# Image-prompt keys projected standing beside the values, then transposed, in a cross-attention kernel

## Chip, cores and metric

The kernel runs on one NeuronCore of one Trainium2 chip. The metric is the device time of one execution in microseconds (us), as the median of several runs; lower is better. Everything is float32. The engines are named as in the profile: PE is the matrix engine (TensorE), PEld its weight loads, DVE the vector engine, ACT the scalar engine, POOL is GpSimd, SP the queue that issues most DMAs.

## What is computed

The reference is one cross-attention layer with image prompts, over a batch of B = 8, with S = 112 queries of C = 320 channels, 20 heads of 16 channels, and a context of T = 375 rows of E = 512 of which the last 4 are image prompts:

```python
text_ehs = encoder_hidden_states[:, :-NUM_TOKENS]
ip_ehs = encoder_hidden_states[:, -NUM_TOKENS:]
q = heads(hidden_states @ W_q)
k_t = heads(text_ehs @ W_k)
v_t = heads(text_ehs @ W_v)
scores_t = jnp.einsum('bhsd,bhtd->bhst', q, k_t) * attn_scale
probs_t = jax.nn.softmax(scores_t, axis=-1)
text_out = jnp.einsum('bhst,bhtd->bhsd', probs_t, v_t)
...
k_ip = heads(ip_ehs @ W_k_ip)
v_ip = heads(ip_ehs @ W_v_ip)
attn_scores = jnp.einsum('bhsd,bhnd->bhsn', q, k_ip) * attn_scale
qsem = jnp.einsum('bhst,bte->bhse', probs_t, text_ehs)
qsem = _l2norm(qsem)
ip_n = _l2norm(ip_ehs)
sem = jnp.einsum('bhse,bne->bhsn', qsem, ip_n)
fused = attn_scores + SEM_SCALE * sem
probs_ip = jax.nn.softmax(fused, axis=-1)
probs_ip = probs_ip * spatial_mask[None, None, :, None]
ip_out = jnp.einsum('bhsn,bhnd->bhsd', probs_ip, v_ip)
...
out = text_out + IP_SCALE * ip_out
out = out @ W_out + b_out
out = out + residual
```

The change concerns only `k_ip` and `v_ip`: the 8 x 4 = 32 prompt rows of all batch items (512 long) times two weights of 512 x 320. Both are computed once, for the whole batch.

## The kernel before

The heads are handled in groups of four (`GROUP`), five groups (`NG`) for each batch item `b`, so there are 40 steps `(b, g)`. A prologue loads and prepares batch item 0. Then the main loop runs over the steps. In a step, `multiplied` issues twelve rounds (`j`) of four matmuls, one for each head of the group, each on its own 32 rows of the array (L673). Between its rounds the scores of the group two steps ahead are computed (`scores`, L624), and the four of them are turned into probabilities (`probabilities`: DVE maximum L637, ACT exponential L641, and a DMA from SP, L646, that lays them out for the DVE transposition of L654, which makes the stationary operand of the following step). The text values and the Gram matrix of the context come in as the moving operand `u`, which SP fills from the doubled Gram matrix (`gram_to_groups`, L460) and POOL with the values (`placed`, L591).

After the rounds, `between(b, g)` issues what prepares the next batch item: the Gram matrix ("inner products") of its context in three blocks of shrinking width (`gram`, L446, 375, 247 and 119 columns, each copied out by ACT at L434), its values (L518), keys (L484), queries (L326). At `b == 0` and `g == 0` it also issues `prompt_projections`, right behind the third block of `gram(1)`.

The order of the instructions of PE, SP, DVE and, in the main loop, ACT is the order of the program text (`manual_schedule`); POOL's is left to a scheduler until the last batch item. The tiles of one tag rotate through their buffers: `bank()` takes one of two banks of PSUM (tag "mm"), so that a tile can only be written when the tile before the last has been read out.

`prompt_projections` before the change works on `ipT`, the 32 prompts standing as columns (four chunks of 128 rows x 32). For the keys, `wkip_sb` is the stationary operand, 128 x 128 at a time: three blocks `i` of output channels by four chunks `e`, each with the 32 prompts as the moving operand (L270). Each block's result, channels x prompts, is copied by ACT into `kip` (L277), and DVE spreads batch item 0's part by heads into `kipb` (L278). The channels of the last block are set apart first, with 16 zeros after each 16 channels, by `spread` on POOL (three copies, L122, and a memset, L123), for which `wkip_sb` is 384 wide. For the values, `ipT` is the stationary operand, 128 x 32, and the 320 channels are the moving one (L287), so that the result stands as prompts x channels; ACT copies it into `vip` (L291), and in step (0, 1) SP sends it to DRAM (`vipd`, L294), from where each batch item's rows are later read back. `kip` is used by `keys(b)` (a POOL copy, L468), and `kipb` by `prompt_logits(0)` in step (0, 3).

Both weights lie in one buffer of the tag "u" (`wip`), which batch item 1's `u` takes over later; they are loaded by two DMAs on SP (L1078 and L1079, recorded under the helper's L116) at the end of the prologue.

Of the kernel before, what the change touches and what calls it, by code (L numbers as in the profile page):

```python
# [8 lines left out]
F32 = mybir.dt.float32  # L9
# [11 lines left out]
def kernel(  # L21
# [14 lines left out]
    nc = tc.nc  # L36
    P = 128
    B, S, C = x.shape
    T, E = ehs.shape[1:]
    H = HEADS  # L40
    D = C // H
# [3 lines left out]
    NE = E // P  # L45
    HC = P // D
    NC = (C + P - 1) // P
    CP = NC * P
    FULL = C // P
# [7 lines left out]
    N = B * NIP  # L57
# [18 lines left out]
    work = ctx.enter_context(tc.tile_pool(name="work", bufs=2))  # L76
# [6 lines left out]
    def bank(name, spare=False):  # L83

        if spare:
            return ps_sc.tile([P, 512], F32, tag="sc", name=name)
        return ps_mm.tile([P, 512], F32, tag="mm", name=name)
# [13 lines left out]
    wv_sb = const.tile([P, NE, C + REST], F32, tag="wv_sb", name="wv_sb")  # L101

    wip = work.tile([P, UCOL], F32, tag="u", name="wip")
    wkip_sb = wip[:, : NE * CP].rearrange("p (e f) -> p e f", f=CP)
    wvip_sb = wip[:, NE * CP : NE * (CP + C)].rearrange("p (e f) -> p e f", f=C)
    wo_sb = const.tile([P, NC, C], F32, tag="wo_sb", name="wo_sb")
    ip_sb = const.tile([N, E], F32, tag="ip_sb", name="ip_sb")
    sm_sb = const.tile([S, 1], F32, tag="sm_sb", name="sm_sb")
# [9 lines left out]
    def spread(eng, t):  # L118

        v = t[:, :, FULL * P :].rearrange("p k (a r d) -> p k a r d", r=2, d=D)  # L120
        for a in (3, 2, 1):
            eng.tensor_copy(v[:, :, a, 0, :], v[:, :, a // 2, a % 2, :])  # L122
        eng.memset(v[:, :, :, 1, :], 0.0)  # L123
# [43 lines left out]
    ident = const.tile([P, P], F32, tag="ident", name="ident")  # L167
# [46 lines left out]
    ipT = const.tile([P, NE, N], F32, tag="ipT", name="ipT")  # L214
    ipnT = const.tile([P, NE, N], F32, tag="ipnT", name="ipnT")
    kip = const.tile([P, NC, N], F32, tag="kip", name="kip")

    kipb = const.tile([P, NC, HC, NIP], F32, tag="kipb", name="kipb")
    vipd = dram.tile([N, C], F32, tag="vipd", name="vipd", bufs=1)
# [43 lines left out]

    def prompt_projections():

        spread(nc.gpsimd, wkip_sb)
        for i in range(NC):
            ps = bank(f"ps_kip{i}")
            for e in range(NE):
                nc.tensor.matmul(  # L270
                    ps[:, :N],
                    wkip_sb[:, e, i * P : (i + 1) * P],
                    ipT[:, e, :],
                    start=(e == 0),
                    stop=(e == NE - 1),
                )
            nc.scalar.copy(kip[:, i, :], ps[:, :N])  # L277
            nc.vector.tensor_tensor(  # L278
                kipb[:, i],
                kip[:, i, :NIP].unsqueeze(1).to_broadcast([P, HC, NIP]),  # L280
                hmask.unsqueeze(2).to_broadcast([P, HC, NIP]),
                ALU.mult,
            )
            yield
        ps = bank("ps_vip")
        for e in range(NE):
            nc.tensor.matmul(  # L287
                ps[:N, :C], ipT[:, e, :], wvip_sb[:, e, :], start=(e == 0), stop=(e == NE - 1)
            )
        vip = work.tile([N, C], F32, tag="vip", name="vip", bufs=1)  # L290
        nc.scalar.copy(vip, ps[:N, :C])  # L291
        yield

        nc.sync.dma_start(vipd, vip)  # L294
        yield


# [131 lines left out]
    def doubled(ps, c):  # L429

        t0 = c * P
        k = min(P, TT - t0)
        g = ug[:, GCOL[c] : GCOL[c] + T - t0]
        nc.scalar.mul(g, ps[:, : T - t0], 2.0)  # L434
        nc.gpsimd.tensor_tensor(g[:, :k], g[:, :k], half[:, :k], ALU.mult)

    def gram(b):

        ctxT = st[b]["ctxT"]

        nc.gpsimd.tensor_copy(ctxT[:, :, TT:T], ipnT[:, :, b * NIP : (b + 1) * NIP])
        for c in range(NT):
            t0 = c * P
            ps = bank(f"ps_g_{b}_{c}")
            for e in range(NE):
                nc.tensor.matmul(  # L446
                    ps[:, : T - t0],
                    ctxT[:, e, t0 : t0 + P],
                    ctxT[:, e, t0:T],
                    start=(e == 0),  # L450
                    stop=(e == NE - 1),
                )
            doubled(ps, c)
            yield
# [536 lines left out]
    def run(key, make, pieces=1):  # L991

        if key not in gens:
            gens[key] = make()
        for _ in range(pieces):
            next(gens[key], None)

    def between(b, g):

        nb = b + 1  # L1000
        new = nb < B


        first = [bs for bs in pairs if bs[0] == (nb if b == 0 else nb + 1)]
        rest = [bs for bs in pairs if bs[0] == nb]
        if g == 0:
            if new:
                run(("g", nb), lambda: gram(nb), 3)
            if b == 0:
                run(("pp",), prompt_projections, NC + 1)  # L1010
            if b > 0 and new:
                run(("f", b - 1), lambda: finish(b - 1))
        if g == 1:
            if new:
                run(("v", nb), lambda: values(nb), 2)
            for bs in first if b == 0 else ():
                run(("q", bs[0]), lambda: project_queries(bs), 3)
        if g == 2 and new:
            run(("v", nb), None)
            run(("k", nb), lambda: keys(nb))  # L1020
            for bs in first if b == 0 else ():
                run(("q", bs[0]), None)
        if g == 2 and b > 0 and new:
            run(("f", b - 1), None, 2)
        if g == 3:
            if new:
                run(("k", nb), None, 1)
            if b > 0 and new:
                run(("f", b - 1), None)
            for bs in first if b > 0 else ():  # L1030
                run(("q", bs[0]), lambda: project_queries(bs), 3)
            if b == 0:
                run(("t", b), lambda: prompt_logits(b))
            for bs in rest:
                run(("q", bs[0]), None)
        if 0 <= g - (b == 0) < NT and nb + 1 < B:
            run(("c", nb + 1), lambda: transposed_context(nb + 1))
        if g == 4:
            if b > 0 and new:
                run(("f", b - 1), None, 2)  # L1040
            if nb < B - 1:
                run(("k", nb), None, 1)
            for bs in (first if b > 0 else []) + rest:
                run(("q", bs[0]), None)
# [49 lines left out]
    for n, (b, g) in enumerate(steps[:-NG]):  # L1094
# [41 lines left out]
        if g == NG - 1 and b < B - 2:  # L1136
            prompt_values(b)
        between(b, g)
        if g == 1:
            values_to_dram(b + 1, nc.sync, 0, 2)  # L1140
# [12 lines left out]
    b = B - 1  # L1153
# [12 lines left out]
    for g in range(NG):  # L1166
# [20 lines left out]
        if g < NG - 1:  # L1187

            n = GROUP - 1 if g <= LEAD else 1
# [36 lines left out]
    last = last_heads(b)  # L1226
# [52 lines left out]
```

## Time and profile before

| what | value |
|---|---|
| median of 3 runs | 442.44 us |
| lowest and highest run | 440.67, 444.03 us |
| profiled execution, first to last instruction | 442.3 us, at a mean granted PE clock of 0.998 |
| DVE, ACT, POOL busy | 325.5, 189.0, 111.7 us |
| rounds of `multiplied`, L673 | 3840 records, 220.5 us of the span |
| DMA | 64.22 MB, mean 145 GB/s |

Of the profiled execution the span is what is recorded; it stands 0.1 us below the median of the runs. In the trace one float32 matmul appears as two records, one for each pass, and a transposition by PE as one. The records of PE overlap, because a matmul's end is modelled and the next one starts before it: what a matmul costs is the distance from one start to the next, not its duration. A shape such as "128*32 128x320" reads: 128 rows and 32 columns of the array, and a moving operand of 128 x 320.

### The profile page before, as it was taken

How to read it: one execution, taken by the hardware profiler on the slowest of the kernel's cores; microseconds unless marked ns; L12 is line 12 of the kernel's file. 1: busy time of each engine (PE TensorE's matmuls, PEld its weight loads, DVE VectorE, ACT ScalarE, POOL GpSimd, SP SyncE). 2: the span in 40 equal slices, each digit the busy share in tenths (PEclk: the TensorE clock that was granted, in tenths of full speed). 3: DMA queues.
4: the chain of work that ended last, by engine and by line, in shares of the span. 5: the costliest groups of instructions: out<-in, count | busy, mean ns of one | idle time of the engine just before them, and what ended most of it. 6: DMA issues, size and time to landing. Idle time of an engine off the chain costs nothing.

```text
span 442.3 us, 12958 instructions
## 1 busy us (share of the span) xinstructions
PE 429.4 (97%) x5024; PEld 330.7 (75%) x5024; DVE 325.5 (74%) x664; ACT 189.0 (43%) x649; POOL 111.7 (25%) x270
## 2 busy tenths in 40 slices
PE   8998999989999999999999999999999999999896
PEld 8857767778777877788777787778777887776784
DVE  4046366886897877887797977977787687878874
ACT  2263233343534353333633453333534253436783
POOL 5302201011142121511142120602124111526440
PEclk9999999999999999999999999999999999999999
DMA  8569965466646756468646746468465527553300
GB/s 249 151 173 254 220 147 151 110 152 126 165 122 166 178 121 162 129 155 159 165 115 163 183 110 164 113 144 199 116 175 139 152 77 197 130 146 105 83 13 27
DMA packets 57995, 64.22 MB, mean 145 GB/s; under 512 B 18432, under 2 KB 52088, under 8 KB 57934
## 3 DMA queue, kind: packets, MB, share of 16 engines
q1 hardware_dynamic: 57494, 62.83, 57.0%
q8 instruction: 40, 0.66, 0.7%
q10 hardware_dynamic: 440, 0.56, 0.4%
q14 instruction: 21, 0.17, 0.1%
HBM read 18.67 MB, written 5.32 MB: 54 GB/s over the span
## 4 chain that ended last, share of the span: by engine, by line
PE 88%; ACT 3%; DMA 3%; DVE 3%; issue 1%; POOL 1%; SPq 0%; POOLq 0%; DVEq 0%
PE ps_qd L673 39%; PE ps_v L518 14%; PE ps_k L484 10%; PE ps_g L446 8%; PE ps_s L624 4%; PE ps_q L326 3%; DMA xg<-p 2%; PE ps_o L883 2%; PE ps_g L418 1%; DVE xgT L654 1%; PE ps_c L388 1%; ACT p L641 1%; PE ps_k L500 1%; DMA ct<-in_ctx_dram 1%; POOL shared L708 1%
## 5 line engine op out<-in xcount | busy, mean ns | idle before, releaser
L673 PE MATMUL ps_qd<-u,xgT 32*112 32x72 f32 (+11 forms) x3840 | 220.5, 353 | 3.2 <-DVE xgT L654 1.3
L673 PEld LDWEIGHTS ps_qd<-u,xgT 32*112 32x112 f32 x3840 | 187.5, 172 | 37.0 <-issue 10.7
L654 DVE STREAM_TRANSPOSE xgT<-xg 128x1536 f32<-128x1536 f32 x40 | 119.1, 2979 | 12.1 <-DMA xg<-p 8.2
L641 ACT ACTIVATE p<-ps_s,nmx 112x371 f32<-112x371 f32 x160 | 87.3, 584 | 86.2 <-DVE nmx L637 69.6
L637 DVE TENSOR_REDUCE nmx<-ps_s 112x1 f32<-112x371 f32 x160 | 77.6, 527 | 50.8 <-PE ps_s L624 49.7
L719 DVE CUSTOM_DVE_ANT_0 junk<-ps_qd,p 112x371 f32<-112x371 f32 x148 | 80.2, 542 | 15.6 <-ACT vext L525 0.5
L624 PE MATMUL ps_s<-kT,qm 32*112 32x375 f32 (+1 forms) x320 | 67.8, 484 | 0.4 <-ACT p L641 0.4
L591 POOL COPY u<-vr 128x64 f32<-128x64 f32 x120 | 25.9, 238 | 151.9 <-PE ps_qd L673 102.3
L518 PE MATMUL ps_v<-wv_sb,ctxT 128*128 128x384 f32 (+1 forms) x192 | 63.5, 480 | 0.0
L518 PEld LDWEIGHTS ps_v<-wv_sb,ctxT 128*128 128x128 f32 x192 | 35.2, 190 | 19.7
L484 PE MATMUL ps_k<-ctxT,wk_sb 128*128 128x371 f32 x136 | 45.9, 482 | 0.0
L686 ACT COPY pvs<-ps_qd 112x21 f32<-112x21 f32 x150 | 16.0, 189 | 65.7 <-PE ps_qd L673 64.8
L446 PE MATMUL ps_g<-ctxT 128*128 128x375 f32 (+2 forms) x168 | 37.6, 380 | 0.0
L484 PEld LDWEIGHTS ps_k<-ctxT,wk_sb 128*128 128x128 f32 x136 | 25.1, 190 | 15.3 <-issue 0.5
L446 PEld LDWEIGHTS ps_g<-ctxT 128*128 128x128 f32 x168 | 28.0, 190 | 8.7 <-ACT ug L434 0.3
L624 PEld LDWEIGHTS ps_s<-kT,qm 32*112 32x112 f32 x320 | 27.1, 170 | 6.3 <-ACT kT L491 2.1
L335 DVE TENSOR_SCALAR qm<-ps_q,emask 128x224 f32<-128x224 f32 (+1 forms) x25 | 9.1, 397 | 20.2 <-PE ps_q L326 20.1
L643 ACT COPY ipl<-ps_s 112x4 f32<-112x4 f32 x140 | 23.8, 170 | 0.0
L525 ACT COPY vext<-ps_v 128x384 f32<-128x384 f32 (+1 forms) x24 | 11.2, 468 | 25.6 <-PE ps_v L518 25.6
L378 DVE STREAM_TRANSPOSE ctxT<-ct 128x512 f32<-128x512 f32 x18 | 19.8, 1103 | 0.1
L491 ACT COPY kT<-ps_k 128x371 f32<-128x371 f32 x17 | 8.0, 469 | 25.3 <-PE ps_k L484 25.3
L858 POOL TENSOR_TENSOR wv<-vip,w 112x1280 f32<-112x1280 f32 x6 | 14.8, 2466 | 15.0 <-DVE w L802 15.0
(160 smaller groups left out, 319.8 us busy)
## 6 DMA issues: line engine op xcount, KB each, us to landing
xg<-p SPq DMA_DIRECT2D x160, 162.3 KB
u<-ug SPq DMA_DIRECT2D x128, 99.0 KB
ct<-in_ctx_dram SPq DMA_DIRECT2D x24, 176.0 KB
vr<-vd SPq DMA_DIRECT2D x32, 120.0 KB
vip<-vipd SPq DMA_DIRECT2D x6, 560.0 KB
vd<-vext SPq DMA_DIRECT2D x7, 320.0 KB
vd<-vext SPq DMA_DIRECT2D x7, 160.0 KB
out_dram<-ob SPq DMA_DIRECT2D x8, 140.0 KB
```

The source lines that it names most:

```text
L378: nc.vector.transpose(ctxT[:, :, c * P : (c + 1) * P].rearrange("p e (j i) -> p j e i", i=RG), ct[:, some, :].rearrange("p j (k e) -> p j ...
L446: nc.tensor.matmul(ps[:, : T - t0], ctxT[:, e, t0 : t0 + P], ctxT[:, e, t0:T], start=(e == 0), stop=(e == NE - 1),)
L484: nc.tensor.matmul(ps[:, :TT], wk_sb[:, e, i * P : (i + 1) * P], s["ctxT"][:, e, :TT], start=(e == 0), stop=(e == NE - 1),)
L518: nc.tensor.matmul(ps[:, :w], ctxT[:, e, c * P : (c + 1) * P], wv_sb[:, e, :w], start=(e == 0), stop=(e == NE - 1),)
L591: nc.gpsimd.tensor_copy(region(b, c)[:, :, UV - c * P :], s["vr"][:, c * QN : (c + 1) * QN, g, :])
L624: nc.tensor.matmul(ps[:S, :w], qm[a * RG : (a + 1) * RG, i, r, j * S : (j + 1) * S], s["kT"][a * RG : (a + 1) * RG, i, :w], start=True, st ...
L637: nc.vector.tensor_reduce(nmx, ps[:S, :TT], AX.X, ALU.max, negate=True)
L641: nc.scalar.activation(p, ps[:S, :TT], AF.Exp, bias=nmx)
L643: nc.scalar.copy(s["ipl"][:, groups[g][a], :], ps[:S, TT:T])
L654: nc.vector.transpose(xT.rearrange("p j (k q) -> p q j k", q=QN), xg.rearrange("p q (j k) -> p q j k", k=RG),)
L673: nc.tensor.matmul(banks[a][:S, j * RG : UW], xT[a * RG : (a + 1) * RG, j, :S], region(b, c)[a * RG : (a + 1) * RG, q, q * RG :], start=(j ...
L719: nc.vector.tensor_tensor_reduce(out=junk, in0=ps[:S, :TT], in1=s["p", g][:, a, :], scale=1.0, scalar=0.0, op0=ALU.mult, op1=ALU.add, accu ...
```

## The change

The keys are projected the way the values are, with the prompts as the stationary operand, and both at once: chunk by chunk, one matmul for the keys into the PSUM partitions 0 to 31 of a bank and one for the values into the partitions 32 to 63 of the same bank, which are two different groups of 32 columns of the array. ACT copies the keys out in two pieces, the second of which sets the last block's channels apart (the zeros between them are written by POOL into the tile `both` beforehand), and the values in a third. Then three PE transpositions, of 32 x 128 each, bring the keys to channels x prompts in one bank, one ACT copy takes them to `kip`, and three DVE instructions make `kipb` as before. `spread` of the weight falls away, and the key weight is 320 wide, loaded as one piece for each partition instead of four.

In `between(0, 0)` the order becomes: two blocks of `gram(1)`, the projections and their three copies, the third block of `gram(1)`, then the transpositions, the copy and the three DVE instructions. The transfer to `vipd` stays in step (0, 1). POOL's scheduler puts the new memset near the start of the program, between the first two instructions that make the identity matrix.

```diff
-    wkip_sb = wip[:, : NE * CP].rearrange("p (e f) -> p e f", f=CP)
-    wvip_sb = wip[:, NE * CP : NE * (CP + C)].rearrange("p (e f) -> p e f", f=C)
+    wkip_sb = wip[:, : NE * C].rearrange("p (e f) -> p e f", f=C)
+    wvip_sb = wip[:, NE * C : 2 * NE * C].rearrange("p (e f) -> p e f", f=C)
...
-        spread(nc.gpsimd, wkip_sb)
-        for i in range(NC):
-            ps = bank(f"ps_kip{i}")
-            for e in range(NE):
+        both = work.tile([2 * N, CP], F32, tag="ipkv", name="ipkv", bufs=1)
+        kp = both[:N]
+        last = kp[:, FULL * P :].rearrange("n (a r d) -> n a r d", r=2, d=D)
+        nc.gpsimd.memset(last[:, :, 1, :], 0.0)
+        ps = bank("ps_ipkv")
+        for e in range(NE):
+            for i, w in enumerate((wkip_sb, wvip_sb)):
                 nc.tensor.matmul(
-                    ps[:, :N],
-                    wkip_sb[:, e, i * P : (i + 1) * P],
+                    ps[i * N : (i + 1) * N, :C],
                     ipT[:, e, :],
+                    w[:, e, :],
                     start=(e == 0),
                     stop=(e == NE - 1),
                 )
-            nc.scalar.copy(kip[:, i, :], ps[:, :N])
+        nc.scalar.copy(kp[:, : FULL * P], ps[:N, : FULL * P])
+        nc.scalar.copy(
+            last[:, :, 0, :], ps[:N, FULL * P : C].rearrange("n (a d) -> n a d", d=D)
+        )
+        nc.scalar.copy(both[N : 2 * N, :C], ps[N : 2 * N, :C])
+        yield
+
+        ps = bank("ps_kip")
+        for i in range(NC):
+            nc.tensor.transpose(
+                ps[:, i * N : (i + 1) * N], kp[:, i * P : (i + 1) * P], ident[:N, :N]
+            )
+        nc.scalar.copy(kip, ps[:, : NC * N].rearrange("p (i n) -> p i n", n=N))
+        for i in range(NC):
             nc.vector.tensor_tensor(
                 kipb[:, i],
...
-            yield
-        ps = bank("ps_vip")
-        for e in range(NE):
-            nc.tensor.matmul(
-                ps[:N, :C], ipT[:, e, :], wvip_sb[:, e, :], start=(e == 0), stop=(e == NE - 1)
-            )
-        vip = work.tile([N, C], F32, tag="vip", name="vip", bufs=1)
-        nc.scalar.copy(vip, ps[:N, :C])
-        yield
-
-        nc.sync.dma_start(vipd, vip)
+        yield
+
+        nc.sync.dma_start(vipd, both[N : 2 * N, :C])
         yield
...
             if new:
-                run(("g", nb), lambda: gram(nb), 3)
+                run(("g", nb), lambda: gram(nb), 2)
             if b == 0:
-                run(("pp",), prompt_projections, NC + 1)
+                run(("pp",), prompt_projections)
+            if new:
+                run(("g", nb), None)
+            if b == 0:
+                run(("pp",), None)
```

## The prediction

> **What bounds the kernel now.** I read first the page's busy times and its chain of work that ended last, then the busy times by stretch.
>
> ```profile
> PE 429.4 (97%) x5024; PEld 330.7 (75%) x5024; DVE 325.5 (74%) x664; ACT 189.0 (43%) x649; POOL 111.7 (25%) x270
> PE 88%; ACT 3%; DMA 3%; DVE 3%; issue 1%; POOL 1%; SPq 0%; POOLq 0%; DVEq 0%
> ```
> ```profile
> 37.20:400.00 362.80, 359.58 (x4347) 276.56 (x4351) 282.79 (x569) 146.53 (x524) 84.78 (x201) 1.00 0.61 150
> ```
>
> The second line is the chain: 88% of the span is PE itself. In the main loop (third line: PE, PEld, DVE, ACT, POOL) PE is idle for 3.2 of 362.8 us. So what the change is worth is the time it takes from PE's own row of work, provided that nothing else comes late behind it. I then read the timeline around the place.
>
> ```profile
> 47.12 0.38 ACT L434 ACTIVATE ug<-ps_g 128x247 f32<-128x247 f32 x1 [1.19 <-PE ps_g L446]
> 47.74 2.77 PE L270 MATMUL ps_kip<-ipT,wip 128*128 128x32 f32 x24
> 50.44 2.34 PE L287 MATMUL ps_vip<-wip,ipT 128*32 128x320 f32 x8
> 51.81 0.11 PEld L287 LDWEIGHTS ps_vip<-wip,ipT 128*32 128x32 f32 x1 [0.16 <-issue]
> 52.08 0.11 PEld L287 LDWEIGHTS ps_vip<-wip,ipT 128*32 128x32 f32 x1 [0.16 <-issue]
> 52.71 0.60 PEld L673 LDWEIGHTS ps_qd<-u,xgT 32*112 32x112 f32 x10 [0.52 <-issue]
> 52.82 0.41 ACT L291 COPY vip<-ps_vip 32x320 f32<-32x320 f32 x1 [2.08 <-PE ps_vip L287]
> ```
>
> The keys hold PE from 47.74 to 50.44, 2.70 us, and the values from 50.44 to 52.71, 2.27 us: 4.97 us between the Gram matrix and the next step's rounds, with no idle in them. The keys' 24 records start 2.70 / 24 = 0.11 us apart, as the Gram matrix's 119-column ones do (eight of mean 274 ns in 1.0 us busy): with only 32 moving columns, the 128x128 weight load sets the pace. The values' loads start 0.27 us apart (51.81, 52.08); there the 320 moving columns do. The eighth record then starts at 52.35 and its slot ends at 52.62, 0.09 us before the next kind of matmul: that is what a change from one array shape to another costs here.
>
> **The new row on PE.** Four chunks by two weights by two passes are 16 records of the values' kind. Eight belong to the keys (columns 0 to 31) and eight to the values (columns 32 to 63). If the two column groups run beside each other, the row takes eight slots: 8 x 0.27 = 2.16 us. There is no matmul in this trace with two column groups at work, so the bounds are 2.16 us (full overlap) and 16 x 0.27 = 4.32 us (none). I take the lower. The nearest row is L673: its four matmuls on four row groups start within 0.01 us of each other and then run together, ten records in 1.22 us.
>
> The Trainium skill ("TensorE: Matmul & The Clock Gate", section "Measured speedup vs the span model") states 2.38 times for three column groups; taken as the same share for two, an estimate, the row would be 2.7 us. The same page ("The mechanism") says that a weight load overlaps a running matmul only if the row group differs, which speaks against this change, since both groups use all rows; by it 16 loads of 0.11 us would stand bare, 3.9 us. The row above disagrees for one column group: the load at 52.08 lies wholly inside the matmuls of a row that starts one every 0.27 us.
>
> Three transpositions follow, of the form of L256 (32*128): there the four records start 0.12 us apart (8.44 to 8.8), so 0.36 us. The array changes shape four times (Gram, projections, Gram, transpositions, rounds) where it changed twice; 4 x 0.09 = 0.36 us. The Gram matrix's third block moves behind the projections at an unchanged price, so it is in neither sum.
>
> The transpositions wait for ACT, because their bank is the projections' bank: all three copies must be done. By L277 (0.19 us for 32 columns) and L291 (0.41 for 320) the copies take 0.36, 0.21 and 0.41, together 0.98 us; they start about 0.16 us after the last slot (a record lasts 0.43, its slot 0.27) plus 0.04 to 0.10 us (L291 and L434 behind their matmuls). That is 1.2 to 1.25 us. PE has as cover the Gram block with two shape changes, 8 x 0.11 + 0.18 = 1.06 us. So PE stands about 0.2 us; without that cover it would stand 1.2.
>
> Sum: 2.16 + 0.36 + 0.36 + 0.2 = 3.1 us for 4.97, **1.9 us off PE's row**. Without overlap it is 5.24, 0.3 us more than before.
>
> **The other engines.** POOL loses the three copies (0.71 us) and the memset (0.31) at 42.16 and gains one memset before the identity is finished. The nearest rows are 0.13 us (128x36 at 37.15); PE's first matmuls would start 0.13 later, but they end 0.16 us before PE can go on ("ps_c" waits for its load until 3.68), so nothing. POOL's next copies for the coming rounds stand behind L733, which waits for the bias load until 49.48, and end at 50.69. The first rounds would start at 50.8; the copies are needed from the fifth round on. ACT has the third Gram copy (L434) behind the three new copies, so POOL's doubling (L435, done at 51.9) and its L468 move little; SP comes for their result only at 58.5. DVE's three L278 come after the copy of `kip`, at about 51.2, before L637 needs DVE at about 52.4.
>
> Both weights must be there at 46.9 instead of 47.7 and 50.4. SP shows when they were:
>
> ```profile
> SPq L646 <- DMA x_sb<-in_x_dram: 1.9, 1, 1.9
> SPq L646 <- DMA wip<-in_L_xattn_W_v_ip_dram: 0.3, 1, 0.3
> ```
>
> SP's third probability transfer of that group is issued at 47.18, after the wait for `x_sb`; the wait for the value weight before it ended at 44.0. The key weight released POOL at 42.16. There are 2.9 us to spare. The key weight's load in 128 pieces of 5 KB instead of 512 of 1.25 KB can only help the loads behind it, which nothing on PE waits for; zero.
>
> **What is late next.** SP's row is not paced by PE from 49.5 to about 74: loads of batch item 2, then `u`, `vd` and probabilities one after another. With PE 1.9 us ahead, the fourth group's probabilities still leave SP at 72.9; the transposition that reads them was at 79.09, and their landing, by the slowest such landing in the chain (84.71 to 88.82, 4.1 us), is by 77.9 against a wish at 77.2. Its result is used only at 84.6. I count nothing. The one long wait of PE in the loop, 1.65 us for ACT before L475 at 93.67, hangs on DVE work that itself starts from PE's queries at 86.58, so it moves along.
>
> The profiled span of 442.3 lies 0.1 below the median of 442.44; 442.4 less 1.9 is **440.5 us**.
>
> **Rivals.**
> 1. The columns do not overlap, wholly or in part: the change does not do what it says. For it speaks that no row of the trace shows such a pair. 0.3 us slower at the worst, 441.5 to 442.7.
> 2. Slower: each of the 15 changes between the two column groups costs what a change of shape costs, 0.09 us, on top of running one after another. 15 x 0.09 = 1.35 with the 0.3 makes 1.6 us, 444.1. It decides from a pair slot of 0.27 + 1.9 / 8 = 0.51 us on; serial alone is 0.54. Against it: the alternating L624 and L673 records on different row groups show no such holes.
> 3. The gain is taken back downstream, by SP's row or by DVE's, where transfers that PE does not pace come no earlier: 442.4. For it: SP issues one transfer after another in that stretch, with few waits. Against it: the slack counted above.
> 4. More than the sum: the earlier loads and POOL's freed 1.0 us shorten a wait such as the 1.65 us: 438.9.
>
> **Numbers.** Forecast 0.55; rivals 0.20, 0.08, 0.11 and 0.06. The forecast's own range is 439.5 to 441.5. The three runs of before lie 3.4 us apart, so a median can sit over a microsecond off; the range reaches over rivals 1 and 3 on the upper side and over rival 4 on the lower: 438.8 to 443.4. One per cent, about what a measurement of this kernel can tell from no change, is 4.4 us, which none of the cases reaches: within 1% 0.87, faster by more 0.08, slower by more 0.05, the two ends for an effect that I don't see.
>
> **What would show it.** Of the changed kernel: the eight records of keys and eight of values starting in pairs, 16 in about 2.2 us of busy time (forecast) or 4.3 (rival 1) or 5.7 (rival 2); a hole of about 0.2 us before the transpositions, put down to ACT; the rounds of step (0, 1) starting near 50.8 instead of 52.71. If they start there and the span is still 442, rival 3 holds, and a new wait of PE after 60 us must show where. Keys' records that start more than 0.27 us apart make the first term wrong.

## The result, and the profile after

| what | before | after |
|---|---|---|
| median of 22 runs each, on the same chip | 443.56 us | 440.65 us |
| lowest and highest run | 440.67, 445.82 us | 438.67, 442.13 us |
| ratio after / before, 95% interval | | 0.9925 [0.9912, 0.9938] |
| span of the profiled execution | 442.3 us | 440.2 us |

By the ratio the change takes 3.3 us off (2.8 to 3.9), by the medians 2.9: faster, by less than 1%. The forecast had 440.5 us, but also 1.9 us of gain from a median of 442.44; with more runs the kernel before lies 1.1 us higher. So it is partly luck that 440.5 is met so closely: its starting point was 1.1 us too low and its gain 1.0 to 1.4 us too small, and the two nearly cancel. A timed value is also not a span: the execution of after that was profiled has a span of 440.2 us and was timed at 441.88, so that a span next to a median, as ahead of the prediction, says little.

Lines of after stand 8 lower in the program from L295 on: L673 is L681, L654 is L662, L646 is L654, L475 is L483, L446 is L454. New are L273 (the 16 projection records), L280, L281 and L284 (their copies), L289 (the transpositions) and L292 (the copy of `kip`). Busy times and chain of after:

```profile
PE 427.9 (97%) x5011; PEld 328.4 (75%) x5011; DVE 326.0 (74%) x664; ACT 188.9 (43%) x649; POOL 110.6 (25%) x267
PE 84%; DMA 5%; ACT 4%; DVE 3%; issue 2%; POOL 1%; SPq 0%; DVEq 0%; POOLq 0%; ACTq 0%
```

PE is still the bound, but the chain now has 84% of PE for 88%, and DMA has risen from 3 to 5%: somewhere a transfer sets the pace now. First the place of the change, in the timeline of after:

```profile
46.34 2.35 PE L273 MATMUL ps_ipkv<-wip,ipT 128*32 128x320 f32 x16
...
46.64 0.12 PEld L273 LDWEIGHTS ps_ipkv<-wip,ipT 128*32 128x32 f32 x2 [0.15 <-issue]
46.91 0.12 PEld L273 LDWEIGHTS ps_ipkv<-wip,ipT 128*32 128x32 f32 x2 [0.15 <-issue]
...
48.62 1.15 PE L454 MATMUL ps_g<-ctxT 128*128 128x119 f32 x8
48.76 0.36 ACT L280 COPY ipkv<-ps_ipkv 32x256 f32<-32x256 f32 x1 [1.88 <-PE ps_ipkv L273]
...
49.24 0.42 ACT L284 COPY ipkv<-ps_ipkv 32x320 f32<-32x320 f32 x1
...
49.71 0.31 PE L289 MATMUL ps_kip<-ident,ipkv 32*128 32x32 f32 x2
49.82 0.59 PE L681 MATMUL ps_qd<-u,xgT 32*112 32x392 f32 x3
49.86 0.22 PE L289 MATMUL ps_kip<-ident,ipkv 32*128 32x32 f32 x1
```

The 16 records start in pairs, one pair every 0.269 us, the two of a pair 7 ns apart; their weight loads come in pairs too, while the pair before still runs. From the first record to the next kind of matmul it is 48.62 - 46.34 = 2.28 us. The last three lines are the part to look at: the step's rounds (L681) start at 49.82, 0.11 us after the first transposition, and the third transposition starts behind the first round. The transpositions hold 32 rows of the array, and the rounds of the other three heads start beside them.

SP's waits for the weights, the answer to the lines shown of before, are of the same kind (1.9 us for `x_sb` and 0.3 for the value weight there), and PE's first record above has no idle time in front of it, so neither weight is late:

```profile
SPq L654 <- DMA wip<-in_L_xattn_W_v_ip_dram: 1.6, 1, 1.6
SPq L654 <- DMA x_sb<-in_x_dram: 1.4, 1, 1.4
```

The step lengths, as distances from one step's first round to the next one's, show where the time went. For each of the two kernels there are two more traces with the same instructions on PE or the same program, from the runs below (a flat load in the kernel before, and it again; a padded load in the changed kernel, and it again):

```
us              before  flat load  again  |  after  padded load  again
step (0,0)       15.50    15.53    15.50  |  13.22     13.22     13.22
(0,1) + (0,2)    23.67    23.67    23.67  |  24.32     23.73     23.85
step (0,4)        8.82     8.78     8.72  |   8.35      8.35      8.35
(0,0) to (0,4)   58.08    58.08    57.99  |  55.98     55.38     55.51
span            442.28   442.31   442.42  | 440.16    439.06    438.69
```

Three things happen: step (0,0) is 2.28 us shorter, always. Step (0,4) is 0.4 us shorter, which nothing in the change explains. And (0,1) with (0,2) is longer by 0.06 to 0.65 us. The experiments take these apart.

### The profile page after: what moved, and what is told of

It reads as the page before. It is cut to its first block, busy times and chain, and to the rows that moved or that the text cites. A ratio compares the mean times of both kernels' runs of the same rounds, so it can differ in the third digit from the quotient of the medians.

```text
span 440.2 us, 12928 instructions
## 1 busy us (share of the span) xinstructions
PE 427.9 (97%) x5011; PEld 328.4 (75%) x5011; DVE 326.0 (74%) x664; ACT 188.9 (43%) x649; POOL 110.6 (25%) x267
## 4 chain that ended last, share of the span: by engine, by line
PE 84%; DMA 5%; ACT 4%; DVE 3%; issue 2%; POOL 1%; SPq 0%; DVEq 0%; POOLq 0%; ACTq 0%
PE ps_qd L681 39%; PE ps_v L526 13%; PE ps_k L492 9%; PE ps_g L454 8%; PE ps_s L632 4%; DMA xg<-p 3%; PE ps_q L334 3%; PE ps_o L891 2%; ACT p L649 2%; DMA vr<-vd 1%; DVE xgT L662 1%; PE ps_g L426 1%; DMA ct<-in_ctx_dram 1%; PE ps_k L508 1%; POOL shared L716 1%
## 5 line engine op out<-in xcount | busy, mean ns | idle before, releaser
L681 PE MATMUL ps_qd<-u,xgT 32*112 32x328 f32 (+11 forms) x3840 | 221.5, 353 | 3.2 <-DVE xgT L662 1.3
L681 PEld LDWEIGHTS ps_qd<-u,xgT 32*112 32x112 f32 x3840 | 188.5, 172 | 36.9 <-issue 10.2
L662 DVE STREAM_TRANSPOSE xgT<-xg 128x1536 f32<-128x1536 f32 x40 | 119.2, 2980 | 14.5 <-DMA xg<-p 9.0
L454 PE MATMUL ps_g<-ctxT 128*128 128x375 f32 (+2 forms) x168 | 37.6, 380 | 0.0
L454 PEld LDWEIGHTS ps_g<-ctxT 128*128 128x128 f32 x168 | 28.0, 190 | 8.8 <-issue 0.5
L442 ACT ACTIVATE ug<-ps_g 128x375 f32<-128x375 f32 (+2 forms) x24 | 9.0, 376 | 22.4 <-PE ps_g L454 17.6
```

Of the source, the lines that this page charges most:

```text
L454: nc.tensor.matmul(ps[:, : T - t0], ctxT[:, e, t0 : t0 + P], ctxT[:, e, t0:T], start=(e == 0), stop=(e == NE - 1),)
L662: nc.vector.transpose(xT.rearrange("p j (k q) -> p q j k", q=QN), xg.rearrange("p q (j k) -> p q j k", k=RG),)
L681: nc.tensor.matmul(banks[a][:S, j * RG : UW], xT[a * RG : (a + 1) * RG, j, :S], region(b, c)[a * RG : (a + 1) * RG, q, q * RG :], start=(j ...
```

## The experiments

**Without the second column group.** In this kernel keys and values go into the same 32 columns, in two banks; all else is as after.

```diff
         ps = bank("ps_ipkv")
+        psv = bank("ps_ipv", spare=True)
...
-                    ps[i * N : (i + 1) * N, :C],
+                    (psv if i else ps)[:N, :C],
...
-        nc.scalar.copy(both[N : 2 * N, :C], ps[N : 2 * N, :C])
+        vip = work.tile([N, C], F32, tag="vip", name="vip", bufs=1)
+        nc.scalar.copy(vip, psv[:N, :C])
...
-        nc.sync.dma_start(vipd, both[N : 2 * N, :C])
+        nc.sync.dma_start(vipd, vip)
```

> The changed kernel, with the value matmuls put into the same 32 columns of the array as the key matmuls (their result goes to a bank of its own), so that nothing can overlap; copies, transpositions, loads and order stay. Theory (the two column groups run beside each other and PE's row is the whole gain): the 16 records start one by one, 0.27 us apart, and the stretch from the first of them to the third Gram block grows from 2.28 to about 4.4 us; the time is 2.1 us above the changed kernel's, that is within 0.3 us of before by the trace, and at most 1 us below before by the timed runs. Rival (the gain comes from the shorter load and POOL's freed time, the columns do not matter): the time stays at the changed kernel's, about 3 us below before.

Measured: 442.58 us, ratio to before 0.9967 [0.9946, 0.9989]. Timeline of PE:

```profile
46.97 0.72 PE L274 MATMUL ps_ipkv<-wip,ipT 128*32 128x320 f32 x2
47.53 0.70 PE L274 MATMUL ps_ipv<-wip,ipT 128*32 128x320 f32 x2
...
51.39 1.15 PE L456 MATMUL ps_g<-ctxT 128*128 128x119 f32 x8
52.47 0.31 PE L291 MATMUL ps_kip<-ident,ipkv 32*128 32x32 f32 x2
```

The records start one by one, 0.269 us apart, and take 51.39 - 46.97 = 4.42 us. Step (0,0) is 15.34 us, 2.12 longer than after. So the overlap of the column groups is 2.12 of the 2.28 us; without it the new way of working is worth 0.16 us in this step. By the ratio this kernel lies 1.5 us below before (0.5 to 2.4), more than the 1 us that was expected at most. The trace shows 0.57 us of that in the first five steps (57.51 for 58.08), 0.49 of it in step (0,4), which is taken up below.

**The load alone, from both sides.** The key weight padded to 384 again in the changed kernel, and the flat, 320 wide key weight in the kernel before, where POOL then sets the last block's channels apart into another place of the buffer.

```diff
-    wkip_sb = wip[:, : NE * C].rearrange("p (e f) -> p e f", f=C)
-    wvip_sb = wip[:, NE * C : 2 * NE * C].rearrange("p (e f) -> p e f", f=C)
+    wkip_sb = wip[:, : NE * CP].rearrange("p (e f) -> p e f", f=CP)
+    wvip_sb = wip[:, NE * CP : NE * (CP + C)].rearrange("p (e f) -> p e f", f=C)
...
-                    w[:, e, :],
+                    w[:, e, :C],
```

This is the edit of the first of the two kernels.

> The changed kernel, with the key weight loaded 384 wide in four pieces for each partition, as before the change. Theory (PE's row is the whole gain): same time as the changed kernel, 2.3 to 3.3 us below before. Rival (a part of the timed gain that the trace of step (0, 0) does not hold, about 0.6 to 1 us, comes from the load in one piece, which lets the loads behind it land earlier): 0.6 to 1 us above the changed kernel, 2 us below before.

> The kernel before, with the key weight loaded 320 wide in one piece, and the last block's channels set apart by POOL into a place of their own (one copy and one memset instead of three copies and a memset); PE's, ACT's and DVE's rows are those of before. Theory: within 0.3 us of before. Rival (load and POOL): 0.6 to 1 us below before.

Measured: 440.44 us, ratio 0.9919 [0.9894, 0.9944], and 443.42 us, 0.9985 [0.9963, 1.0007]. The steps in the table above do not know the difference. The first ratio speaks against the rival (3.6 us below before, 2.5 at the least, where the rival had 2). The second does not decide by itself: 0.7 us below before, with an interval from 1.6 below to 0.3 above. So the load in one piece and POOL's work are worth nothing that the steps show, and nothing that is clear of the noise in the times.

**Without the cover of the Gram block.** The third block goes back in front of the projections.

```diff
-                run(("g", nb), lambda: gram(nb), 2)
+                run(("g", nb), lambda: gram(nb), 3)
             if b == 0:
-                run(("pp",), prompt_projections)
-            if new:
-                run(("g", nb), None)
-            if b == 0:
-                run(("pp",), None)
+                run(("pp",), prompt_projections, 2)
```

> The changed kernel, with all three Gram blocks ahead of the projections, so that the transpositions come directly behind the projections and nothing covers the copies of ACT. Theory: PE stands between the last projection and the first transposition for what the copies take, 0.8 to 1.2 us (the values' copy need not be waited for here, because the banks rotate differently), less one change of array shape: 0.7 to 1.1 us above the changed kernel. Rival (the order does not matter, since the next step's rounds go on their own row groups): same time as the changed kernel.

Measured: 440.93 us, ratio 0.9932 [0.9908, 0.9955]; step (0,0) 13.67 us, 0.45 more than after. Timeline of PE:

```profile
48.09 2.35 PE L273 MATMUL ps_ipkv<-wip,ipT 128*32 128x320 f32 x16
50.92 0.37 PE L289 MATMUL ps_kip<-ident,ipkv 32*128 32x32 f32 x3 [0.49 <-ACT ipkv L280]
51.13 1.22 PE L681 MATMUL ps_qd<-u,xgT 32*112 32x392 f32 x10
```

Uncovered, PE stands 0.49 us, not the 1.2 of the working: by this line it waits for the key copies. It does not wait for the value copy, which starts at 51.00, behind the first transposition (in this order the transpositions take the Gram block's bank, not the projections'). So the cover is worth 0.45 us against this order, less than the 0.7 to 1.1 that were expected; the 1.2 us of the working, with all three copies waited for, does not arise here.

**The kernel before once more,** as a control of the comparison.

> The kernel before, unchanged, as a second profile and a control of the comparison. The step table of the traces so far accounts for 2.75 us of gain (2.28 in step (0, 0), 0.47 in front of step (1, 0)), the timed ratio for 3.3. Theory (the first profile of before was a lucky one, above all in batch item 6, where it took 0.5 to 1.4 us less than five other traces): this profile's span is about 443.2 us, with 31 us instead of 29.98 for the three steps (6, 0) to (6, 2); the ratio holds 1. In front of step (1, 0) the step (0, 4) takes 8.8 us again, with the load of instructions (queue 8) starting 0.1 to 0.3 us before that step's first round. Rival (the 0.47 us is chance): 8.3 us here.

Measured: 443.13 us, ratio 0.9993 [0.9969, 1.0017]. Two copies of one program agree to 0.3 us here. The span of the second profile is 442.42 us, where 443.2 was expected. Its step (0,4) lasts 8.72 us, near the 8.82 of the first, so its length is not chance, as the rival had it.

**Step (0,4): which transfer is late?** In the kernel before, DVE's transposition of that step (L654) stands in its queue for a landing of probabilities, and PE stands behind it before L475. Timelines of DVE and PE, before and then after:

```profile
89.68 2.95 DVE L654 STREAM_TRANSPOSE xgT<-xg 128x1536 f32<-128x1536 f32 x1 [0.41 <-issue]
...
93.67 0.54 PE L475 MATMUL ps_k<-ident,k 128*128 128x128 f32 x3 [1.65 <-ACT ipl L643]
```
```profile
86.95 2.97 DVE L662 STREAM_TRANSPOSE xgT<-xg 128x1536 f32<-128x1536 f32 x1
...
90.97 0.54 PE L483 MATMUL ps_k<-ident,k 128*128 128x128 f32 x3 [1.18 <-ACT ipl L651]
```

Against the step's first round (86.47 and 84.23) the transposition starts at 3.21 and at 2.72 us: 0.49 earlier, and PE's wait shrinks by 1.65 - 1.18 = 0.47. That the transposition of before waits for a semaphore shows in its line among DVE's queue entries (shortest, median and longest in ns, then the first and the last start): the longest, the one at 88.2, lasts until the transposition starts.

```profile
L654 DVEq EVENT_SEMAPHORE  x4: 21/35/1453, 78.0 to 88.2; - x4
```

The DMA view of the last 0.3 us before the step's first round, before and then after, names a suspect (queue, kind, packets, MB, share of 16 engines):

```profile
q1 hardware_dynamic: 27, 0.04, 78.6%
q8 instruction: 1, 0.02, 42.2%
```
```profile
q1 hardware_dynamic: 31, 0.05, 73.0%
```

In the kernel before, a 16 KB packet with instructions (queue 8) starts 0.17 us before the step's first round and takes 1.82 us, while the probabilities are on their way; in after it starts 0.50 us behind that round and holds up none of them. The packet records of the two traces show it directly. The probabilities of the last two transfers are 224 packets of 1484 bytes. In before the last eight of them start one after another from 1.64 us behind the first round on, just as the instruction packet ends (1.65), and the last is done at 2.61; in after the last is done at 0.65. Such packets of instructions come one every 8 to 17 us in this stretch, as the engines go through the program. So the theory: the change shortens the program, which shifts these packets against the steps. Two kernels test it, which leave the prompts' work alone and only change the number of small matmuls that keep PE busy at the start (their results are used by nothing): seven more than in after, and five fewer than in before.

```diff
-        for _ in range(n):
+        for _ in range(11 if n == 4 else 0):
+            nc.tensor.matmul(ps[:RG, :48], ident[:, :RG], ident[:, :48], start=True, stop=True)
+        for _ in range(0 if n == 4 else n):
             nc.tensor.matmul(ps[:, :P], ident, ident, start=True, stop=True)
```
```diff
-        for _ in range(n):
-            nc.tensor.matmul(ps[:, :P], ident, ident, start=True, stop=True)
+        nc.tensor.matmul(
+            ps[:, : n * P].rearrange("p (k q) -> p k q", q=P),
+            ident,
+            ident.unsqueeze(1).to_broadcast([P, n, P]),
+            start=True,
+            stop=True,
+        )
```

> The changed kernel, with the four warm-up matmuls at the start of PE's row replaced by eleven smaller ones, 7 more, which is about as many instructions as the change took out of PE's row ahead of step (0, 1). Theory (the change moved PE's load of instructions by about 0.7 us against the work, out of the way of a probability transfer, and this is the 0.47 us): the load starts before the first round of step (0, 4) again, the transposition L654 in that step waits for its transfer, and the step takes 8.8 us; step (0, 0) stays at 13.2. Rival (the 0.47 us comes from the new row itself, for instance from PE being ahead of SP): 8.35 us.

> The kernel before, with the seven warm-up matmuls at the start of PE's row replaced by two wide ones of the same work, so that PE's row is 5 matmuls shorter from the start. Theory of the instruction load: it starts about 0.5 us later against the work, behind the transfer, and the step (0, 4) takes 8.3 to 8.4 us with step (0, 0) at 15.5 as before. Rival: 8.8 us as before.

Measured: the changed kernel with the longer program has its packet 0.13 us ahead of the first round and a step (0,4) of 8.62 us (8.8 expected); the kernel before with the shorter one has it 0.83 us behind, and a step of 8.35 (8.3 to 8.4 expected). Step (0,0) stays at 13.22 and 15.50. Over all 14 traces of this study the rule holds without exception:

```
packet's start against the step's first round, us -> length of step (0,4), us
-0.21 8.72   -0.20 8.78   -0.17 8.82   -0.15 9.47   -0.13 8.62
+0.13 8.36   +0.50 8.35   +0.50 8.33   +0.52 8.34   +0.52 8.36   +0.53 8.33   +0.80 8.35   +0.81 8.35   +0.83 8.35
```

The 9.47 has a second cause, taken up with its kernel below. In each of the five traces of the upper row the last eight of the 224 packets start within 0.02 us of the instruction packet's end; in the nine others all 224 are done by 0.83 us. So the mechanism is shown in the step. In the times it can hardly be: 440.63 us, 0.9942 [0.9919, 0.9964], and 443.75 us, 0.9995 [0.9973, 1.0018]; the effect of 0.3 to 0.5 us is below these intervals.

**Four column groups, split by chunks.** Half of the keys' sum in each of two groups, the values' halves in the other two; the halves of the sum are put together by matmuls against two identities on top of each other, in place of the transpositions.

```diff
...
+        for r in range(2):
+            for h in range(2):
+                nc.tensor.matmul(
+                    ps[h * N : (h + 1) * N, :C],
+                    ipT[:, 2 * h + r, :],
+                    wkip_sb[:, 2 * h + r, :],
...
-            nc.tensor.transpose(
-                ps[:, i * N : (i + 1) * N], kp[:, i * P : (i + 1) * P], ident[:N, :N]
+            nc.tensor.matmul(
+                ps[:, i * N : (i + 1) * N], kp[:, i * P : (i + 1) * P], two, start=True, stop=True
```

> The changed kernel on four groups of 32 columns: the keys' four chunks are shared out to two groups (two chunks each), the values' 320 channels to two groups (160 channels each); instead of the three transpositions, three matmuls against two identities above each other add the two halves of the keys. Theory (all column groups run beside each other, whatever their number): the stretch of projections falls from 2.28 to about 1.15 us; the copies of ACT then start 1.1 us earlier, and the Gram block of 1.1 us still covers them but for 0.1 us; with the doubled records of the three matmuls, 0.8 to 1.1 us below the changed kernel, 439.7 us. Rival (two groups at most run beside each other, or the loads of the weights set the pace): 2.2 us again and the changed kernel's time or 0.2 us above it.

Measured: 441.1 us, ratio 0.9947 [0.9927, 0.9967]; step (0,0) 12.83 us. Timeline of PE:

```profile
47.36 1.15 PE L471 MATMUL ps_g<-ctxT 128*128 128x119 f32 x8
48.44 0.85 PE L303 MATMUL ps_kip<-two,ipkv 64*128 64x32 f32 x6
49.22 1.22 PE L698 MATMUL ps_qd<-u,xgT 32*112 32x392 f32 x10
```

Four groups do run beside each other: the projections take 1.22 us (46.13 to 47.36). But what replaces the transpositions has two passes on 64 rows, holds the rounds back for 0.78 us instead of 0.11, and eats most of it. The step is 0.39 us shorter than the changed kernel's, where 0.8 to 1.1 was expected, and the times show none of it (the ratio is not below the changed kernel's 0.9925).

**The order of issue.** All keys, then all values, in two column groups.

```diff
-        for e in range(NE):
-            for i, w in enumerate((wkip_sb, wvip_sb)):
+        for i, w in enumerate((wkip_sb, wvip_sb)):
+            for e in range(NE):
```

> The changed kernel with its 16 projection records in another order: all eight of the keys (columns 0 to 31), then all eight of the values (columns 32 to 63). If the overlap of two column groups needs neighbours in the order of issue to lie on different groups (PE takes its instructions strictly in order), only the seam overlaps: the 16 records take about 4.2 us (one-column-group kernel: 4.42) instead of 2.28, step (0,0) lasts about 15.1 us and the time is about 442.5. If each column group has a queue of its own, the records still take about 2.3 us and step (0,0) 13.2.

Measured: 441.03 us, ratio 0.9942 [0.992, 0.9963]; step (0,0) 14.29 us. Neither expectation holds: the records take 49.61 - 46.23 = 3.38 us, half way between. The weight loads in the timeline tell how:

```profile
46.53 0.11 PEld L273 LDWEIGHTS ps_ipkv<-wip,ipT 128*32 128x32 f32 x1 [0.16 <-issue]
46.80 0.11 PEld L273 LDWEIGHTS ps_ipkv<-wip,ipT 128*32 128x32 f32 x1 [0.16 <-issue]
47.07 0.11 PEld L273 LDWEIGHTS ps_ipkv<-wip,ipT 128*32 128x32 f32 x1 [0.16 <-issue]
47.34 0.68 PEld L273 LDWEIGHTS ps_ipkv<-wip,ipT 128*32 128x32 f32 x7 [0.16 <-issue]
```

Up to 47.07 one load comes every 0.27 us, from 47.34 to 47.90 two. The single records say the same: the first of the values starts at 47.340, 7 ns behind the fifth of the eight of the keys; so the second group waits until about four records lie ahead of it, no longer, and then runs along. By the spacing of the records the last three of the keys (47.603 to 48.141) start behind the first of the values, though they stand ahead of it in the program: across column groups the order of issue is not kept strictly, as the expectation had supposed.

**Four column groups, split by channels.** Keys 0 to 127, keys 128 to 319, and the values' halves, each with its whole sum, so that the transpositions stay as they are; those of the second and third block lie on rows 32 to 63 and in a bank of their own. It is followed by the changed kernel once more, on the same chip.

```diff
...
+        hw = C // 2
+        parts = (
+            (wkip_sb, 0, P),
+            (wkip_sb, P, C),
+            (wvip_sb, 0, hw),
+            (wvip_sb, hw, C),
+        )
         for e in range(NE):
-            for i, w in enumerate((wkip_sb, wvip_sb)):
+            for i, (w, lo, hi) in enumerate(parts):
                 nc.tensor.matmul(
-                    ps[i * N : (i + 1) * N, :C],
+                    ps[i * N : (i + 1) * N, : hi - lo],
...
```

> The changed kernel with four column groups instead of two, split by output channels: keys 0 to 127, keys 128 to 319, values 0 to 159, values 160 to 319, each over all four chunks; the transpositions stay in one pass (rows 0 to 31 for the first block, rows 32 to 63 for the other two, in two banks), kip takes two ACT copies and vipd two transfers. If a slot of four records costs what the widest costs (192 columns, about 0.16 us by 0.27 x 192 / 320), the projections take eight slots, 1.3 us plus a change of shape, 0.9 to 1.0 us less than the 2.28 of the changed kernel; the transpositions cost about 0.11 us as there, and step (0,0) lasts about 12.3 us instead of 13.22; time 439.7 to 440. If the transpositions on different row groups or the second bank cost a wait, it shows as a PE gap before the rounds of (0,1) and step (0,0) stays above 12.8.

> The changed kernel once more, unchanged, timed on the same chip and against the same runs of before as the four-group kernel. If the 2.75 us of the traces (2.28 in step (0,0), 0.47 in step (0,4)) are the whole effect, the ratio is 0.994; if something the steps do not show adds 0.5 us or more, it stays at 0.9925 or lower. Step (0,0) 13.2 us, step (0,4) 8.35.

Measured: 441.91 us (439.7 to 440 expected), ratio 0.9958 [0.9936, 0.998], against 440.25 us, 0.9917 [0.9895, 0.994], for the changed kernel once more. This second ratio is on the side of an effect that the steps do not show (0.9925 or lower), but its interval reaches 0.994. In the four-group kernel the projections take 1.42 us (46.26 to 47.68) and step (0,0) 12.27, as expected, 0.95 below the changed kernel's. But step (0,4) takes 9.47 us instead of 8.35. The instruction packet lies 0.15 us ahead of the first round again, as in the kernel before. Timeline of PE, and busy times by stretch (PE, PEld, DVE, ACT, POOL, granted clock):

```profile
90.12 0.54 PE L501 MATMUL ps_k<-ident,k 128*128 128x128 f32 x3 [1.66 <-ACT ipl L669]
```
```profile
91.01:94.42 3.41, 3.41 (x17) 2.04 (x19) 1.56 (x6) 0.15 (x1) 0.28 (x1) 0.50 0.74 185
```

PE stands 1.66 us, and behind it the granted clock is 0.50 for 3.41 us. That costs step (0,4) 0.6 us more than the packet did in the kernel before, and step (1,0) 0.3 (11.65 instead of 11.35). In all 14 profiles the recorded clock rises and falls a whole number of times 3.413 us apart (here it is full for 85.33 us, 25 of them, before it falls). The stand of 1.66 us lies whole inside one such stretch, 87.60 to 91.01; that of 1.65 us in the kernel before is split over two, 0.48 and 1.17 us. That would explain why the clock stayed full there, but it is a single case and was not tested.

**The same with five instructions fewer at the start,** by the edit shown above for the shorter program.

> The four-group kernel split by channels, with the seven matmuls on the identity at the start of the program issued as two wider ones (five matmuls fewer, the same columns of work), as in the earlier kernel with the shorter program. Step (0,0) was 12.27 us there, 0.95 less than in the changed kernel, but step (0,4) was 9.47 instead of 8.35: the 16 KB load of instructions started 0.15 us before the step's first round, the transposition of DVE started late, PE stood 1.66 us, and the granted clock then fell to half from 91.01 to 94.42 us. Theory: with five instructions fewer the load starts about 1 us later against the rounds, 0.8 to 0.9 us into the step; step (0,4) goes back to 8.35, step (1,0) from 11.65 to 11.35, the clock stays whole, step (0,0) stays 12.27, and the time is 0.9 us below the changed kernel's, a ratio of about 0.990 and a median near 439.4. Rival: the four groups themselves, or the earlier start of the step, make the transfer late; then step (0,4) stays above 9 and the time near 441.9.

Measured: the packet starts 0.52 us behind the first round (0.8 to 0.9 expected), step (0,4) is 8.36 us, step (1,0) 11.35, the clock stays at 1.00: as expected. Yet the time is 441.54 us, ratio 0.9935 [0.9911, 0.996], 2 us above the expectation (by the ratio, 1.6). In the profile the gain is lost above all in step (0,1), which takes 13.01 us instead of the 11.91 to 12.23 of before and after. Timelines of DVE, ACT and PE:

```profile
56.55 2.97 DVE L685 STREAM_TRANSPOSE xgT<-xg 128x1536 f32<-128x1536 f32 x1 [4.26 <-DMA ct<-in_ctx_dram]
...
59.36 0.94 DVE L668 TENSOR_REDUCE nmx<-ps_s 112x1 f32<-112x371 f32 x2
...
59.89 1.03 ACT L672 ACTIVATE p<-ps_s,nmx 112x371 f32<-112x371 f32 x2 [4.45 <-DVE nmx L668]
60.81 0.86 ACT L556 COPY vext<-ps_v 128x384 f32<-128x384 f32 x2
...
61.34 1.28 PE L344 MATMUL ps_x<-ident,x_sb 112*128 112x112 f32 x6 [0.92 <-ACT vext L556]
```

Read upwards: PE waits for the copy of the values' bank, which stands on ACT behind an exponential, which waits for DVE's maximum, which stands behind a transposition that waits for a landing. The chains of this kernel and of after name the transfer (start, length):

```profile
49.13 6.88 DMA xg<-p
```
```profile
48.91 6.60 DMA xg<-p
```

In both the probabilities land at 55.5 to 56.0, the loads of batch item 2's context issued right behind them. (The timeline puts the end of DVE's wait down to such a load; what the transposition reads is the probabilities.) In the kernel before, DVE comes to that transposition without a wait; in after it waits. Timelines of DVE, before and then after:

```profile
55.27 2.98 DVE L654 STREAM_TRANSPOSE xgT<-xg 128x1536 f32<-128x1536 f32 x1
```
```profile
56.07 2.96 DVE L662 STREAM_TRANSPOSE xgT<-xg 128x1536 f32<-128x1536 f32 x1 [3.65 <-DMA ct<-in_ctx_dram]
```

What such a wait costs depends on how late in step (0,1) the transposition starts. Over all 14 traces:

```
start of the transposition against step (0,1)'s first round, us -> length of (0,1) + (0,2), us
2.55 23.67   2.94 23.67   3.31 23.75   4.10 23.67   4.36 23.67   4.83 23.73   5.39 23.67   5.40 23.73   5.60 23.69
5.69 23.78   5.77 23.85   5.95 24.03   6.24 24.33   7.00 25.09
```

Up to a start of about 5.6 us nothing is lost but 0.08 us, beyond it one microsecond for each microsecond. Counted from the first round of step (0,0), the transposition starts 18.0 to 20.0 us later in all 14, without an order by kernel, and not at the same time in two executions of one program (19.46 and 18.99 us in the changed kernel). So a shorter step (0,0) uses up room: in the four traces of the kernel before and its variants 1.2 to 3.1 us were left. The landing takes up to 0.65 us of the changed kernel's gain in (0,1) and (0,2), and 1.4 of the 3.2 us that this kernel gains in step (0,0) in its one profile, which has the latest start of all; whether its other executions lose as much is not shown. In the changed kernel's second profile the chain in that stretch runs through PE but for one ACT copy of 0.49 us. No version beat the changed kernel clearly: the lowest ratios, 0.9917 and 0.9919, are those of its own repetition and of the padded load.

## Why the prediction was right, and where not

**The bound** was read rightly: in the loop PE is idle 2.6 us of 361.4 in after as well.

```profile
36.60:398.00 361.40, 358.80 (x4334) 275.00 (x4338) 283.18 (x569) 146.59 (x526) 83.70 (x197) 1.00 0.61 151
```

**The overlap of the columns,** the term that decided: 8 x 0.269 = 2.15 us for a forecast of 2.16, with the change of shape 2.28. The kernel with one column group gives the other bound, 4.42 against 4.32, and 442.58 us, within rival 1's 441.5 to 442.7. Rival 2's price for a change of group is not there: a pair on two groups takes 0.269 us, a single record on one group as much. Two groups run together as fast as one, not at the 2.7 us that was estimated from the 2.38 times in "Measured speedup vs the span model" of the Trainium skill ("TensorE: Matmul & The Clock Gate"); the 7 ns between the two of a pair are nearer to that section's own span model, about 4 ns for each further tile. The loads lie behind running matmuls although both groups use all rows, against the sentence of "The mechanism" that the prediction used. The prediction misread one row by little: the four records of L673 start within 0.02 us (52.711 to 52.731), not 0.01; nothing rests on it.

**The transpositions and the wait for ACT** are the mis-sized terms. Three transpositions were priced at 3 x 0.12 from a row where they follow each other; here they cost 0.11 us in all, because the next rounds start beside them, which the working had left out. The 0.2 us of waiting for ACT is not there: the transpositions start 1.08 to 1.09 us after the Gram block's start, in after (49.71 - 48.62) as in the kernel with one column group (52.47 - 51.39). So PE's new row is 4.97 - 2.28 = 2.69 us, where the working had 3.1, and 1.9 us of gain became 2.28 in step (0,0).

**"I count nothing" for what is late next** failed, both ways. The landing in step (0,1) was not looked at: the working followed the probabilities that leave SP at 72.9, which are read at 79.09, in step (0,3). The third group's, read in step (0,1), were the ones with little slack: 1.2 to 3.1 us, and PE came 2.28 us earlier (up to 0.65 us back). The slowest landing that the working allowed for was 4.1 us; this one took 6.60 in after. And of the 1.65 us before L475 it said that it "moves along" with PE's queries; it does not, because the DVE work there waits for a landing that an instruction packet delays. That is rival 4, with a cause that was not thought of: 0.4 us of the gain came from where the packet fell, which is luck. By the traces the first five steps are 2.4 us shorter (58.05 to 55.62, means of three traces each).

**What stays open.** Those three traces each differ by 3.0 us in span (442.34 to 439.30), the timed runs by 3.3 [2.8, 3.9]. The remaining 0.6 to 0.9 us lies, as far as the traces show it, in the prologue, where the granted clock of PE is full from 4.6 to 7.7 us on in different executions, and in steps of later batch items that wait for transfers; from (5,4) to (6,2) the same kernel takes 39.9 to 40.9 us. It was not settled whether the change has a part in that.

## What to carry to other kernels

Where a small stationary operand leaves columns of the array empty, put a second product there and alternate the two in the order of issue: here the two together took 2.28 us, and the values alone 2.27 before. After a gain on the bounding engine, look for the first transfer that this engine does not pace and ask how long before its use it lands; that slack, not the engine's idle time, is what the gain can use, and it is to be read from several executions, since landings move between them. And a step that changes although the edit does not touch it may owe this to where the program's own loads fall: count the instructions before you explain it otherwise.

## What the runs showed of the hardware

- Column groups: neighbours on different groups start 7 ns apart; two groups took 2.28 us for 16 records, one group 4.42. In blocks of eight, the second group joins when about four records of the first remain.
- Single-pass transpositions on 32 rows hold up the next row-tiled matmuls little (0.02 to 0.21 us for three; 0.11 in after); two-pass matmuls on 64 rows hold them up for 0.78 us. Whether the passes or the rows decide was not tested.
- A 16 KB packet of instructions takes 0.9 to 1.9 us. In five traces the last eight packets of a transfer started only as it ended, 1.42 to 1.64 us into the step, and the engine that waited for them was 0.3 to 0.5 us later. Five to seven matmuls more or fewer at the start of the program decided whether this happened.
- After a stand of 1.66 us in one kernel the granted clock was 0.50 for 3.41 us; after one of 1.65 us in the kernel before it was not. The first lies in one of the stretches of 3.41 us between which the recorded clock changes, the second in two; that this decides is not shown.
